# Two-layer transformer on one core: layer 1's weighted expert rows turned by DMA transposes of 16-bit halves instead of TensorE, with small moves of stores and copies between queues and steps

## The chip, the cores and the metric

The kernel runs on one core of one Trainium2 chip. The metric is the device time of one execution in microseconds, given as the median of several runs. One program holds both layers; nothing runs on the host.

## The reference

The input is x of shape (4, 512, 512): four sequences (b) of 512 rows, 2048 rows in all. Each of two layers computes a plain layernorm and adds two branches to x: attention and a mixture of experts, both fed by the normed rows.

```python
xn = layernorm(x)
x = x + L0_attn(xn) + L0_ffn(xn)
xn = layernorm(x)
x = x + L1_attn(xn) + L1_ffn(xn)
```

Layer 0's attention has 16 heads of 128. For each it makes queries and local keys (each normed and rotated), local values, a window of 128 keys and the block before it, and a sparse branch: every four rows are compressed to one entry, and each query takes the best 8 of the 128 compressed entries. Layer 0's experts: top 2 of 8, each a 512 x 512 product, weighted sum. Layer 1's attention is a plain softmax over 512 keys with 16 heads of 32. Layer 1's experts, which the main part of the change touches, end in a projection:

```python
h = einsum('td,edf->etf', xf, expert_w) + expert_b     # 8 experts, top 2 used
combined = sum of silu(h) of the two chosen experts, weighted by the softmax of their scores
out = combined @ proj_w + proj_b
y = x + out
return norm_w * y / sqrt(mean(y * y) + eps)            # x here is the normed xn
```

## The kernel before

All values are f32. The 2048 rows are 16 tiles n of 128 rows (NT = 16); 512 columns are four chunks of 128 (KC = 4). Each engine runs a fixed order of instructions. The order is found when the kernel is built, by a scheduler; instructions given to `keep_in_program_order` stay in the order in which the program issues them, the others may be moved. Transfers are issued from three engines' orders (SP, ACT, POOL); a transfer whose input is not ready holds everything behind it in that order. Tiles come from pools with a number of buffers each (`bufs`), and a new tile waits until the old one's users are done.

**Layer 0** runs in 32 steps of a pair of heads g and a sequence b. A step projects queries, keys and values (`p`, L734, through sums `u` on DVE), norms them (`squares`, L601 to L616), turns them for the products (trq L758, trk L772, trc L931 on TensorE, or stores of 16-bit halves `halves_q`, `halves_c` (L692), `halvesd_q`, `halvesd_c` (L698) and DMA transposes), then makes scores (L845, L856), contexts (L906 to L911, scaled by ACT at L922) and output products (L939, L970). Other work is hung into the steps by place: a list of pairs (step, place within it) and function, with places 0, 1, 2, 3, 3.5 and 4 in a step. Among it:

- Steps 2 to 4, preparation for layer 0's experts: `load_whole` loads a tile of normed rows (`xw`), `part_halves` copies it on ACT so that the low and the high 16-bit halves lie apart (`xh`, L1087), `store_parts` writes that to DRAM. [...]
- Steps 5 to 23, the experts: gathers of rows by POOL (L489, L524), stores (`xrd_r<-xr_r`, L529) and DMA transposes (`xT_r<-xrd_r`, L534), products `hp_r` (L552).
- Each step copies 16 KB of compressed entries (`cv0s`) at its head.
- Steps 29 to 31, `next_layer` for tiles 0 to 11: the rows of layer 1's layernorm (`xn`, L247) are stored (`xnd`, L250), POOL adds a bias to the residual `acc` (L1149), and `acc` is stored to DRAM (`accd`, L1150). Tiles 12 to 15 follow at the start of layer 1.

**Layer 1** runs in 64 slots (a row tile g and a quarter kc of the heads). A slot makes scores (L1522), exponentials on ACT (L1524), the product with the values (L1536), and part of the queries for a later tile (L1482, L1498). The experts lie over slots 9 to 47. From slot 48 on comes the mixing of tile n, one stage a slot, at slots s - 1 to s + 3 with s = 48 + 13 n // 16, so that tiles 0 and 1, 5 and 6, 10 and 11 share a slot:

- `fetch_mix`: POOL gathers the two experts' rows of each token, `g0` and `g1` (L569).
- `mix`: DVE weights and adds them (L1638, L1639) into `g0`.
- `turn_mix`: a load of the normed rows `xa` (L1645), four TensorE transposes `trc` (L1648), a load of the residual (`bring`, L1590), and an ACT copy into `combT` with a factor 0.5 (L1652).
- `project_mix`: four products `po` (L1660) of `combT` with the projection, DVE adds `xa` (L1661), ACT squares (L1664), POOL makes the root (L1665, L1666).
- `finish_mix`: DVE scales (L1671) and adds to the residual (L1594); SP stores to `out` (L1597), or to `accd` (L1599) where attention's part is still to come.

Of the kernel before, what the change touches and what calls it, by code (L numbers as in the profile page):

```python
# [12 lines left out]
F32 = mybir.dt.float32  # L13
# [37 lines left out]
def two_layers(ctx: ExitStack, tc: tile.TileContext, a: dict, out: bass.AP, large: bass.AP):  # L51
# [37 lines left out]
    def load_block(g, nm):  # L89


        w = wpool.tile([P, KC, 3 * D], F32, tag=nm, name=f"{nm}_{g}", bufs=1 if nm == "wA" else 2)
        for f in range(2):
            nc.sync.dma_start(out=w[:, ts(f, 2), :],
                              in_=a[nm][g, ts(f, 2 * P), :].rearrange("(k p) c -> p k c", p=P))
        return w
# [124 lines left out]
        tc.keep_in_program_order(V.memset(turned, 1.0))  # L221
        V.tensor_scalar(turned[R:P, :], wcol[R:P, 0:1], wcol[R:P, 1:2], D * math.sqrt(D), ALU.mult, ALU.mult)

    def layernorm(n, pool, bank, scaled=False, bufs=None):

        pin = tc.keep_in_program_order if n < TC else (lambda x: x)
        st = small.tile([P, 6], F32, tag="st", name=f"st_{n}")
        made_ = V.bn_stats(st, acc[:, n, :])  # L230
        if n < 2 * TC:
            tc.keep_in_program_order(made_)
        mv = small.tile([P, 2], F32, tag="mv", name=f"mv_{n}")
        V.bn_aggr(mv, st)
        V.tensor_scalar(mv[:, 1:2], mv[:, 1:2], 1e-5, None, ALU.add)
        G.tensor_tensor(mv[:, 1:2], mv[:, 1:2], nhalf[:, 0:1], ALU.pow)
        if scaled:
            G.tensor_scalar(mv[:, 0:1], mv[:, 0:1], mv[:, 1:2], -1.0, ALU.mult, ALU.mult)
        made = {}

        def rows():
            tag = "ctx" if n in (2, 3) else "xn"
            xn = made["xn"] = (wk0 if n in (2, 3) else pool).tile([P, HID], F32, tag=tag, name=f"xn_{n}", bufs=bufs)
            if scaled:
                pin(A.activation(xn, acc[:, n, :], AF.Identity, scale=mv[:, 1:2], bias=mv[:, 0:1]))
            else:
                made_ = V.tensor_scalar(xn, acc[:, n, :], mv[:, 0:1], mv[:, 1:2], ALU.subtract, ALU.mult)  # L247
                if n < TC or n + 1 == NT:
                    tc.keep_in_program_order(made_)
            (nc.scalar if TC <= n < 2 * TC else nc.sync).dma_start(out=xnd[ts(n, P), :], in_=xn)  # L250

        def turn():
            xn, tr = made["xn"], bank("tr", f"trx_{n}")
            for k in range(KC):
                made_ = pin(PE.transpose(tr[:, ts(k, P)], xn[:, ts(k, P)], ident))
                if n == TC + 1:
                    tc.keep_in_program_order(made_)
            pin(A.copy(xnT[:, :, ts(n, P)], tr.rearrange("p (k t) -> p k t", k=KC)))
        return rows, turn


# [205 lines left out]
    class Experts:  # L467
# [95 lines left out]
        def gather(self, n):  # L563

            rs = []
            for k in range(2):
                x = self.pool.tile([P, HID], F32, tag=f"row{k}", name=f"row{k}_{self.r.name}_{n}",
                                   bufs=(4, 3)[k] if self.silu else None)
                G.indirect_dma_start(out=x, out_offset=None, in_=self.yd,  # L569
                                     in_offset=at_rows(self.r.slot[:, k, n : n + 1]))  # L570
                rs.append(x)
            return rs
# [17 lines left out]
    for t_ in cv0s:  # L590
        G.memset(t_, 0.0)
        G.memset(t_[96:P, D : D + 1], 2.0)

    def squares(x, heads, pool, name, extra=1.0, use="k"):

# [482 lines left out]
    whole = {}  # L1078

    def load_whole(n):  # L1080
        x = whole[n] = rout["halves"].tile([P, HID], F32, tag="xw", name=f"xw_{n}", bufs=4)
        nc.sync.dma_start(out=x, in_=xnd[ts(n, P), :])

    def part_halves(n):
        x = whole[n]
        xh = whole[n] = rout["halves"].tile([P, 2, HID], U16, tag="xh", name=f"xh_{n}", bufs=4)
        A.copy(xh, x.bitcast(U16).rearrange("p (d h) -> p h d", h=2))  # L1087

    def store_parts(n):
        tc.keep_in_program_order(nc.sync.dma_start(out=xhd[ts(n, P)], in_=whole.pop(n)))  # L1090
# [29 lines left out]
    for b, place in enumerate(((3, 4), (4, 0), (4, 1), (4, 2), (4, 3))):  # L1120
        if b:
            jobs0.append((place, lambda b=b: rout["r"].list(b - 1)))
        if b < B:
            jobs0.append((place, lambda b=b: rout["r"].mark(b)))
    there = [(2, 4)] + [(3, h) for h in (0, 1, 2, 3, 3.5, 4)] + [(4, h) for h in (0, 1, 2)]
    for n in range(NT):
        k = n // 2
        for d, f in enumerate((load_whole, part_halves, store_parts)):
            jobs0.append((there[k + d], lambda n=n, f=f: f(n)))
    jobs0.append(((4, 3), begin_experts))  # L1130
    jobs0.append(((4, 3.5), lambda: rout["ex"].store_halves(0)))
    jobs0.append(((4, 3.5), lambda: rout["ex"].fetch_halves(1)))
# [8 lines left out]
            jobs0.append((at[2 * i + 1], lambda i=i: rout["ex"].fetch(i + 1)))  # L1141
        jobs0.append((at[2 * i + 1], lambda i=i: rout["ex"].store_halves(i + 2)))
    def next_layer(n, pool, bank):
        make_rows, turn_ = layernorm(n, pool, bank, bufs=2 if bank is psum else TC)

        def rows():
            make_rows()

            G.tensor_tensor(acc[:, n, :], acc[:, n, :], rout["wo_b"], ALU.add)  # L1149
            nc.sync.dma_start(out=accd[ts(n, P), :], in_=acc[:, n, :])  # L1150
        return rows, turn_

    v = {}
# [132 lines left out]
    for i, (g, b) in enumerate(steps):  # L1286
# [6 lines left out]
        turn_last = turn_keys  # L1293
        now = qkT
        cT = qp.tile([P, HG, S], F32, tag="cT", name=f"cT_{g}_{b}", bufs=1)
        nc.sync.dma_start(out=cv0s[i % 2][96:P, 0:D], in_=cv[0:32, b, 0:D])
        em0, lT0 = scores(i, 0, now, (lambda: (turn_last(1), next(comp[0]))) if i == 0 else None)
        if i:
            turn_last(1)
        if more:  # L1300
            load_sums(i + 1)
            qkT, sums_x, first, second, third, fourth, fifth, turn_queries, turn_keys, _ = project(i + 1)
            first()
            sums_x()
            if b == 2 and g + 1 in groups:
                groups[g + 1][0][0] = load_block(g + 1, "wA")
        run0((i, 0))
        em1, lT1 = scores(i, 1, now)
        if i == 0:
# [313 lines left out]
    def begin_mixing():  # L1623
        scratch.close()
        rout["mix"] = scratch.enter_context(tc.tile_pool(reuse_waits="tile", name="mix", bufs=2, side="right"))
        rout["ex1"].pool = rout["mix"]
        load_square(rout["mix"], "pw")
        for nm in ("pb", "nw1"):
            rows[nm] = load(rout["mix"], nm, [P, HID], a[nm].partition_broadcast(P))

    def fetch_mix(n):

# [2 lines left out]
    def mix(n):  # L1635

        g0, g1 = held[n]
        tc.keep_in_program_order(V.tensor_scalar(g0, g0, r1.gate[:, 0, n : n + 1], None, ALU.mult))  # L1638
        V.scalar_tensor_tensor(g0, g1, r1.gate[:, 1, n : n + 1], g0, ALU.mult, ALU.add)  # L1639
        held[n] = g0  # L1640

    def turn_mix(n):
        g0 = held[n]
        x = rout["mix"].tile([P, HID], F32, tag="xr", name=f"xa_{n}", bufs=4)
        nc.sync.dma_start(out=x, in_=xnd[ts(n, P), :])  # L1645
        tr = bank1("mm", f"trc_{n}")
        for f in range(KC):
            PE.transpose(tr[:, ts(f, P)], g0[:, ts(f, P)], ident)  # L1648
        bring(n, 1)
        cT_ = rout["mix"].tile([P, KC, P], F32, tag="xT", name=f"combT_{n}", bufs=3)  # L1650

        A.activation(cT_, tr.rearrange("p (k t) -> p k t", k=KC), AF.Copy, scale=0.5)  # L1652
        held[n] = cT_, x

    def project_mix(n):
# [833 lines left out]
```

## Time and profile before

| | us |
|---|---|
| median of 3 runs | 1981.68 |
| lowest, highest | 1981.44, 1984.95 |
| profiled execution, its own time | 1975.01 |
| its span in the profile | 1973.2 |

In the profiled execution TensorE's clock was 0.999 of full speed. Busy times of the stages that the change touches, from the windows of the trace:

| stretch, us | what runs | PE busy | ACT busy | DMA share |
|---|---|---|---|---|
| 160 to 210 | preparation of halves | 48.90 of 50 | 35.02 | 0.60 |
| 1290 to 1340 | end of layer 0 | 44.95 of 50 | 23.35 | 0.40 |
| 1870 to 1890 | mixing | 20.00 of 20 | 7.54 | 0.51 |

How to read the profile: PE is TensorE's products, PEld its weight loads beside them, DVE, ACT and POOL the other engines, SP only issues transfers. A group's row gives line, engine, operation, result and operands, count, then the busy time (overlaps of the group counted once), mean duration of one in ns, and the idle time of the engine ahead of the group with what ended it. A row of a timeline gives start, length, engine, line, operation and count, and in brackets the idle time before it with its releaser; SPq and ACTq rows are transfers as their queue issues them. A row of transfer issues ends with the median time from issue to landing.

### The profile page before, as it was taken

What the parts mean: (1) busy time and instruction counts of PE and PEld (TensorE: products, weight loads), DVE (VectorE), ACT (ScalarE), POOL (GpSimd) and SP (SyncE); (2) the same over time, 40 slices, a digit from 0 to 9 for tenths busy, and PEclk for the clock granted to TensorE, in tenths of its full rate; (3) what the DMA queues carried; (4) which work ended last, traced back from release to release, by engine and by line L of the source; (5) the groups of instructions that cost most, each with busy time, mean ns of one, the idle gap of its engine ahead of it and who ended that gap; (6) DMA issues with size and microseconds to landing.
All of it is one profiled execution on the core that took longest, in us unless ns stands there. A gap on an engine that the chain in (4) does not pass through costs nothing.

```text
span 1973.2 us, 28229 instructions
## 1 busy us (share of the span) xinstructions
PE 1933.4 (98%) x9010; PEld 1206.8 (61%) x9010; DVE 1481.5 (75%) x3662; ACT 892.8 (45%) x2650; POOL 756.1 (38%) x827
## 2 busy tenths in 40 slices
PE   7999999999999999999999999999999999999998
PEld 4676667776677677766667776666434445445443
DVE  7778878786776777776668888888796655666886
ACT  5556654444444444444445455455233433333332
POOL 5423244443433333344332454455114432333551
PEclk9999999999999999999999999999999999999999
DMA  9214366654666575567663433333317775775541
GB/s 293 104 61 142 130 176 180 198 155 144 186 191 167 172 204 152 147 184 223 221 223 98 121 109 109 95 113 105 122 53 257 256 256 191 277 251 175 158 154 67
DMA packets 224589, 326.51 MB, mean 165 GB/s; under 512 B 110384, under 2 KB 144304, under 8 KB 212656
## 3 DMA queue, kind: packets, MB, share of 16 engines
q1 hardware_dynamic: 196208, 173.60, 30.3%
q0 software_dynamic: 27072, 148.91, 22.4%
q10 hardware_dynamic: 1152, 2.10, 0.3%
q8 instruction: 74, 1.21, 0.3%
q14 instruction: 83, 0.68, 0.1%
HBM read 230.44 MB, written 70.25 MB: 152 GB/s over the span
## 4 chain that ended last, share of the span: by engine, by line
PE 79%; DVE 10%; DMA 4%; ACT 3%; issue 2%; POOL 1%; SPq 0%; DVEq 0%; ACTq 0%; POOLq 0%
PE p L734 23%; PE hp_r L552 12%; PE op L939 4%; PE st L856 4%; PE st L1522 3%; PE po L1660 3%; PE cx L1536 3%; PE qp L1498 3%; PE sp L845 2%; PE ox L970 2%; PE o L1605 2%; DMA halvesd_q<-halves_q 2%; PE oz L970 1%; PE ca L908 1%; PE trk L772 1%
## 5 line engine op out<-in xcount | busy, mean ns | idle before, releaser
L552 PE MATMUL hp_r<-we_r,xT_r 128*128 128x512 f32 (+1 forms) x592 | 226.4, 596 | 1.2 <-DMA we_r<-in_Wh,wrow_r 0.8
L606 POOL TENSOR_TENSOR ss_q<-ss_q,nhalf 128x4 f32<-128x4 f32 x64 | 70.9, 1108 | 375.0 <-ACT ss_q L603 375.0
L864 POOL TENSOR_TENSOR lT<-lT,lmask 128x512 f32<-128x512 f32 (+1 forms) x128 | 150.7, 1191 | 102.9 <-ACT lT L860 101.8
L734 PE MATMUL p<-wT,x 128*128 128x384 f32 x512 | 176.6, 488 | 2.6 <-DVE u L800 1.5
L734 PE MATMUL p<-wB,x 128*128 128x384 f32 x512 | 176.9, 490 | 1.3 <-DVE u L814 1.0
L734 PE MATMUL p<-wA,xnT 128*128 128x384 f32 x512 | 173.6, 490 | 1.0 <-DVE u L782 1.0
L860 ACT ACTIVATE lT<-st,ss_k 128x256 f32<-128x256 f32 (+1 forms) x256 | 98.8, 441 | 158.6 <-PE st L856 155.4
L1524 ACT ACTIVATE pT<-st 128x1024 f32<-128x1024 f32 x128 | 123.4, 1016 | 59.6 <-PE st L1522 51.1
L552 PEld LDWEIGHTS hp_r<-we_r,xT_r 128*128 128x128 f32 (+1 forms) x592 | 83.6, 170 | 98.2 <-issue 92.8
L734 PEld LDWEIGHTS p<-wB,x 128*128 128x128 f32 x512 | 94.0, 191 | 64.7 <-issue 8.8
L734 PEld LDWEIGHTS p<-wT,x 128*128 128x128 f32 x512 | 93.4, 190 | 64.9 <-DVE s L880 4.8
L734 PEld LDWEIGHTS p<-wA,xnT 128*128 128x128 f32 x512 | 95.1, 192 | 60.8 <-DVE u L782 2.8
L601 ACT ACTIVATE sq_q<-qb 128x128 f32<-128x128 f32 x256 | 79.2, 310 | 96.4 <-DVE qb L788 53.0
L856 PE MATMUL st<-qkT 128*128 128x256 f32 (+1 forms) x512 | 114.6, 353 | 0.0
L569 POOL DMA_INDIRECT row_r<-yd,slot_r x64 | 72.5, 1133 | 74.5 <-DMA yd<-yr_r 21.8
L856 PEld LDWEIGHTS st<-qkT 128*128 128x128 f32 x512 | 92.2, 190 | 11.5 <-issue 1.8
L939 PE MATMUL op<-Wo,cT 128*128 128x512 f32 x208 | 92.8, 593 | 0.0
L752 ACT ACTIVATE qb<-qb,ss_q 128x128 f32<-128x128 f32 x256 | 81.8, 392 | 21.3 <-POOL ss_k L605 16.0
L606 POOL TENSOR_TENSOR ss_k<-ss_k,nhalf 128x2 f32<-128x2 f32 (+1 forms) x96 | 86.7, 903 | 8.0
L734 PE MATMUL p<-wT,xnT 128*128 128x384 f32 x256 | 88.2, 487 | 0.3 <-DVE wT L121 0.3
L489 POOL DMA_INDIRECT xr_r<-xnd,rows_r x36 | 40.5, 1125 | 120.6 <-PE trm_r L540 88.4
L922 ACT ACTIVATE ctx<-cb,sums 128x128 f32<-128x128 f32 x128 | 39.7, 360 | 101.0 <-DVE sums L918 93.6
(390 smaller groups left out, 4558.5 us busy)
## 6 DMA issues: line engine op xcount, KB each, us to landing
x<-xsd SPq DMA_DIRECT2D x112, 256.0 KB, 5.1
yd<-yr_r SPq DMA_DIRECT2D x72, 256.0 KB, 5.4
xrd_r<-xr_r SPq DMA_DIRECT2D x36, 256.0 KB, 2.3
halvesd_c<-halves_c SPq DMA_DIRECT2D x27, 256.0 KB, 3.5
halvesd_q<-halves_q SPq DMA_DIRECT2D x26, 256.0 KB, 2.9
wA<-in_wA SPq DMA_DIRECT2D x16, 384.0 KB, 3.8
wB<-in_wB SPq DMA_DIRECT2D x16, 384.0 KB, 6.8
xnd<-xn SPq DMA_DIRECT2D x24, 256.0 KB, 2.0
```

The costliest lines, as they stand in the source:

```text
L552: PE.matmul(hp[ts(h, m), :], lhsT=xT[:, k, ts(h, m)], rhs=w[:, ts(k, HID)], start=(k == 0), stop=(k == KC - 1))
L569: G.indirect_dma_start(out=x, out_offset=None, in_=self.yd, in_offset=at_rows(self.r.slot[:, k, n : n + 1]))
L601: pin(A.activation(sq, x[:, h, :], AF.Square, accum_out=ss[:, j : j + 1]))
L606: pin(G.tensor_tensor(ss, ss, nhalf[:, 0:n], ALU.pow))
L734: fixed(PE.matmul(p, lhsT=x[:, k, ts(c, P)], rhs=w[:, k, :], start=(k == 0), stop=(k == 1)))
L752: A.activation(x[:, j, :], x[:, j, :], AF.Copy, scale=scale[:, n : n + 1])
L856: PE.matmul(st[:, ds((t % 2) * 256, n)], lhsT=qkT[:, HG + h, ts(t, P)], rhs=qkT[:, h, ds(t * P, n)], start=True, stop=True)
L860: A.activation(lT[:, ds(half * 512 + c * 256, n)], st[:, ds(c * 256, n)], AF.Exp, scale=norm_k[(i, h)][2 * half + c])
L864: G.tensor_tensor(dst, dst, lmask.rearrange("p a w j -> p (a w j)")[:, 0:n], ALU.mult)
L939: PE.matmul(op, lhsT=cT[:, h, ts(t, P)], rhs=wo[:, h, :], start=(h == 0), stop=(h == HG - 1))
L970: PE.matmul(p[:, ts(c, 256)], lhsT=left[:, ts(c, P)], rhs=right, start=new and c == 0, stop=True, skip_group_check=True)
L1524: A.activation(pt[:, ts(pair, 2), :], st, AF.Exp, scale=SCALE1)
```

## The change

1. The weighted rows of layer 1's experts are no longer turned by TensorE. `mix` copies `g0` on ACT into the buffer of `g1` with its 16-bit halves apart, and stores that to DRAM (`mhd`, two buffers) from SP. `turn_mix` issues a DMA transpose from there into `combT`. The factor 0.5 is put on the gates once. The second operation of the mix is kept in program order, and the numbers of buffers of the two gathered rows are swapped from 4 and 3 to 3 and 4.
2. The small copies of entries (`cv0s`) are issued a step ahead from step 5 on.
3. In `next_layer` for tiles 0 to 11 the stores of `xnd` and `accd` are issued from ScalarE's queue instead of SP's (for `xnd`, tiles 4 to 7 were there already).
4. The preparation of halves for layer 0's experts gets other places: tiles 0 to 5 in steps 1 and 2, in a pool of their own with two buffers, the rest from step 2 to step 4. The ACT copies are kept in program order.

```diff
@@ -221,7 +221,7 @@
         tc.keep_in_program_order(V.memset(turned, 1.0))
         V.tensor_scalar(turned[R:P, :], wcol[R:P, 0:1], wcol[R:P, 1:2], D * math.sqrt(D), ALU.mult, ALU.mult)
 
-    def layernorm(n, pool, bank, scaled=False, bufs=None):
+    def layernorm(n, pool, bank, scaled=False, bufs=None, on_scalar=False):
 
 
 
@@ -247,7 +247,7 @@
                 made_ = V.tensor_scalar(xn, acc[:, n, :], mv[:, 0:1], mv[:, 1:2], ALU.subtract, ALU.mult)
                 if n < TC or n + 1 == NT:
                     tc.keep_in_program_order(made_)
-            (nc.scalar if TC <= n < 2 * TC else nc.sync).dma_start(out=xnd[ts(n, P), :], in_=xn)
+            (nc.scalar if TC <= n < 2 * TC or on_scalar else nc.sync).dma_start(out=xnd[ts(n, P), :], in_=xn)
 
         def turn():
             xn, tr = made["xn"], bank("tr", f"trx_{n}")
@@ -565,7 +565,7 @@
             rs = []
             for k in range(2):
                 x = self.pool.tile([P, HID], F32, tag=f"row{k}", name=f"row{k}_{self.r.name}_{n}",
-                                   bufs=(4, 3)[k] if self.silu else None)
+                                   bufs=(3, 4)[k] if self.silu else None)
                 G.indirect_dma_start(out=x, out_offset=None, in_=self.yd,
                                      in_offset=at_rows(self.r.slot[:, k, n : n + 1]))
                 rs.append(x)
@@ -590,6 +590,9 @@
     for t_ in cv0s:
         G.memset(t_, 0.0)
         G.memset(t_[96:P, D : D + 1], 2.0)
+
+    def load_first_entries(i):
+        nc.sync.dma_start(out=cv0s[i % 2][96:P, 0:D], in_=cv[0:32, steps[i][1], 0:D])
 
     def squares(x, heads, pool, name, extra=1.0, use="k"):
 
@@ -1078,13 +1081,13 @@
     whole = {}
 
     def load_whole(n):
-        x = whole[n] = rout["halves"].tile([P, HID], F32, tag="xw", name=f"xw_{n}", bufs=4)
+        x = whole[n] = (rout["halves"] if n >= 6 else sp0).tile([P, HID], F32, tag="xw", name=f"xw_{n}", bufs=4 if n >= 6 else 2)
         nc.sync.dma_start(out=x, in_=xnd[ts(n, P), :])
 
     def part_halves(n):
         x = whole[n]
-        xh = whole[n] = rout["halves"].tile([P, 2, HID], U16, tag="xh", name=f"xh_{n}", bufs=4)
-        A.copy(xh, x.bitcast(U16).rearrange("p (d h) -> p h d", h=2))
+        xh = whole[n] = (rout["halves"] if n >= 6 else sp0).tile([P, 2, HID], U16, tag="xh", name=f"xh_{n}", bufs=4 if n >= 6 else 2)
+        tc.keep_in_program_order(A.copy(xh, x.bitcast(U16).rearrange("p (d h) -> p h d", h=2)))
 
     def store_parts(n):
         tc.keep_in_program_order(nc.sync.dma_start(out=xhd[ts(n, P)], in_=whole.pop(n)))
@@ -1122,11 +1125,11 @@
             jobs0.append((place, lambda b=b: rout["r"].list(b - 1)))
         if b < B:
             jobs0.append((place, lambda b=b: rout["r"].mark(b)))
-    there = [(2, 4)] + [(3, h) for h in (0, 1, 2, 3, 3.5, 4)] + [(4, h) for h in (0, 1, 2)]
+    there = [((1, 4), (2, 0), (2, 1)), ((2, 0), (2, 1), (2, 2)), ((2, 1), (2, 2), (2, 3)), ((2, 4), (3, 0), (3, 1)),
+             ((3, 0), (3, 1), (3, 2)), ((3, 1), (3, 2), (3, 3)), ((3, 4), (4, 0), (4, 1)), ((4, 0), (4, 1), (4, 2))]
     for n in range(NT):
-        k = n // 2
-        for d, f in enumerate((load_whole, part_halves, store_parts)):
-            jobs0.append((there[k + d], lambda n=n, f=f: f(n)))
+        for place, f in zip(there[n // 2], (load_whole, part_halves, store_parts)):
+            jobs0.append((place, lambda n=n, f=f: f(n)))
     jobs0.append(((4, 3), begin_experts))
     jobs0.append(((4, 3.5), lambda: rout["ex"].store_halves(0)))
     jobs0.append(((4, 3.5), lambda: rout["ex"].fetch_halves(1)))
@@ -1141,13 +1144,13 @@
             jobs0.append((at[2 * i + 1], lambda i=i: rout["ex"].fetch(i + 1)))
         jobs0.append((at[2 * i + 1], lambda i=i: rout["ex"].store_halves(i + 2)))
     def next_layer(n, pool, bank):
-        make_rows, turn_ = layernorm(n, pool, bank, bufs=2 if bank is psum else TC)
+        make_rows, turn_ = layernorm(n, pool, bank, bufs=2 if bank is psum else TC, on_scalar=bank is psum)
 
         def rows():
             make_rows()
 
             G.tensor_tensor(acc[:, n, :], acc[:, n, :], rout["wo_b"], ALU.add)
-            nc.sync.dma_start(out=accd[ts(n, P), :], in_=acc[:, n, :])
+            (nc.scalar if bank is psum else nc.sync).dma_start(out=accd[ts(n, P), :], in_=acc[:, n, :])
         return rows, turn_
 
     v = {}
@@ -1293,7 +1296,8 @@
         turn_last = turn_keys
         now = qkT
         cT = qp.tile([P, HG, S], F32, tag="cT", name=f"cT_{g}_{b}", bufs=1)
-        nc.sync.dma_start(out=cv0s[i % 2][96:P, 0:D], in_=cv[0:32, b, 0:D])
+        if i < 5:
+            load_first_entries(i)
         em0, lT0 = scores(i, 0, now, (lambda: (turn_last(1), next(comp[0]))) if i == 0 else None)
         if i:
             turn_last(1)
@@ -1304,6 +1308,8 @@
             sums_x()
             if b == 2 and g + 1 in groups:
                 groups[g + 1][0][0] = load_block(g + 1, "wA")
+            if i >= 4:
+                load_first_entries(i + 1)
         run0((i, 0))
         em1, lT1 = scores(i, 1, now)
         if i == 0:
@@ -1627,6 +1633,7 @@
         load_square(rout["mix"], "pw")
         for nm in ("pb", "nw1"):
             rows[nm] = load(rout["mix"], nm, [P, HID], a[nm].partition_broadcast(P))
+        tc.keep_in_program_order(V.tensor_scalar(r1.gate, r1.gate, 0.5, None, ALU.mult))
 
     def fetch_mix(n):
 
@@ -1636,20 +1643,18 @@
 
         g0, g1 = held[n]
         tc.keep_in_program_order(V.tensor_scalar(g0, g0, r1.gate[:, 0, n : n + 1], None, ALU.mult))
-        V.scalar_tensor_tensor(g0, g1, r1.gate[:, 1, n : n + 1], g0, ALU.mult, ALU.add)
-        held[n] = g0
+        tc.keep_in_program_order(V.scalar_tensor_tensor(g0, g1, r1.gate[:, 1, n : n + 1], g0, ALU.mult, ALU.add))
+        h = g1.bitcast(U16).rearrange("p (h d) -> p h d", h=2)
+        tc.keep_in_program_order(A.copy(h, g0.bitcast(U16).rearrange("p (d h) -> p h d", h=2)))
+        held[n] = dram.tile([P, 2, HID], U16, tag="mhd", name=f"mhd_{n}", bufs=2)
+        tc.keep_in_program_order(nc.sync.dma_start(out=held[n], in_=h))
 
     def turn_mix(n):
-        g0 = held[n]
+        cT_ = rout["mix"].tile([P, KC, P], F32, tag="xT", name=f"combT_{n}", bufs=3)
+        tc.keep_in_program_order(nc.sync.dma_start_transpose(out=cT_.bitcast(U16), in_=held[n].rearrange("p h d -> (p h) d")))
         x = rout["mix"].tile([P, HID], F32, tag="xr", name=f"xa_{n}", bufs=4)
         nc.sync.dma_start(out=x, in_=xnd[ts(n, P), :])
-        tr = bank1("mm", f"trc_{n}")
-        for f in range(KC):
-            PE.transpose(tr[:, ts(f, P)], g0[:, ts(f, P)], ident)
         bring(n, 1)
-        cT_ = rout["mix"].tile([P, KC, P], F32, tag="xT", name=f"combT_{n}", bufs=3)
-
-        A.activation(cT_, tr.rearrange("p (k t) -> p k t", k=KC), AF.Copy, scale=0.5)
         held[n] = cT_, x
 
     def project_mix(n):
```

## The prediction

> **What bounds the kernel now.** I read the profile page first (engine shares and slices), then the waits, then the windows and the timelines of the four stretches that the edits touch: about 160 to 260 us (preparation of halves), 1290 to 1390 us (border of the layers), and 1815 to 1948 us (mixing).
>
> ```profile
> span 1973.2 us, 28229 instructions
> ...
> PE 1933.4 (98%) x9010; PEld 1206.8 (61%) x9010; DVE 1481.5 (75%) x3662; ACT 892.8 (45%) x2650; POOL 756.1 (38%) x827
> ...
> PE   7999999999999999999999999999999999999998
> ...
> PEclk9999999999999999999999999999999999999999
> ```
>
> TensorE (PE) has work in 98% of the span at full clock. Only 1973.2 - 1933.4 = 39.8 us are left without it, of which about 15 lie in the first slices and 7 in the last. So an edit can gain in two ways only: PE instructions fall out of a stretch where PE is full, or one of the few PE stalls closes. The chain of waits says the same (PE 79% of the span, the first layer's projection and experts ahead). Losses have no such limit: any operand that comes late becomes time. The windows show where PE is full:
>
> ```profile
> 160.00:210.00 50.00, 48.90 (x242) 33.50 (x241) 41.00 (x146) 35.02 (x100) 12.24 (x16) 1.00 0.60 186
> 210.00:260.00 50.00, 47.27 (x234) 32.00 (x235) 46.23 (x146) 26.90 (x95) 16.14 (x19) 0.97 0.31 102
> ...
> 1290.00:1340.00 50.00, 44.95 (x221) 31.07 (x220) 42.63 (x116) 23.35 (x77) 28.28 (x30) 1.00 0.40 122
> 1340.00:1390.00 50.00, 48.77 (x242) 31.33 (x241) 39.43 (x119) 23.46 (x72) 21.71 (x24) 1.00 0.47 143
> ...
> 1890.00:1910.00 20.00, 20.00 (x90) 9.50 (x89) 17.48 (x25) 7.17 (x13) 14.03 (x13) 1.00 0.62 200
> ```
>
> The second number is the length, then busy time of PE, weight loads, DVE, ACT, POOL; then clock and DMA share. PE lacks 3.8 us in the early stretch, 6.3 us at the border, nothing in mixing.
>
> **Part 1, the turn of the weighted rows.** Removed from PE are 64 transposes:
>
> ```profile
> L1648 PE MATMUL trc<-ident,row_r 128*128 128x128 f32 x64 | 9.3, 273 | 0.2 <-DVE qk L1511 0.2
> ```
>
> Their records overlap, so 64 x 273 ns would be too much. In the timeline a group of four starts at 1844.28 and the next line follows at 1844.81: 0.53 us. Ten single tiles at 0.53, two double ones at 0.96 and the first pair at 1.43 (with its 0.24 of idle) make 8.65 us. PE is full there, so all of it comes off if nothing else is late.
>
> What takes their place: per tile one ACT copy of 128x1024 16-bit words (1.05 us by the halves_q row, for the 0.59 us combT copy removed), one store of 256 KB, one DMA transpose. ACT gains 16 x 0.45 = 7 us at under 50% load and has idle of 5 to 6.5 us in each slot, so its load costs nothing; its copy now stands between the two exponentials of a slot and waits for DVE's mix, but the attend product uses the previous slot's exponentials, so some 8 us cover it. Cost appears where a product po (L1660) waits for combT. The nearest rows for the transfers are
>
> ```profile
> x<-xsd SPq DMA_DIRECT2D x112, 256.0 KB, 5.1
> ...
> xrd_r<-xr_r SPq DMA_DIRECT2D x36, 256.0 KB, 2.3
> ...
> xnd<-xn SPq DMA_DIRECT2D x24, 256.0 KB, 2.0
> ```
>
> and for the transposes of the same shape
>
> ```profile
> xT_r<-xrd_r SPq DMA_TRANSPOSE x36, 4.9
> ```
>
> of which single ones landed 3.2 us after issue where nothing else ran, 9.4 at worst. From mix to combT this is 1.05 + 2.0 + 3.2 = 6.3 us at least, 8.3 at the median of the transpose, with 0.3 for each issue. Between the end of the mix on DVE and po there are 12 to 13.5 us for single tiles in before, but 6.9 (n=0), 10.6 (n=5), 10.3 (n=10), 8.4, 6.8, 7.4 (n=13 to 15). The chain alone would mostly fit.
>
> It does not run alone: it is in SP's queue, and in the compiled order of the changed kernel most transposes of tile n stand behind the store of the finished tile n-2 (n-3 in places), which holds SP until DVE has finished that tile.
>
> ```profile
> 1853.88 0.34 SPq L1597 DMA_DIRECT2D out<-acc  x1
> ...
> 1863.49 0.34 SPq L1597 DMA_DIRECT2D out<-acc  x1
> ...
> 1902.23 0.34 SPq L1597 DMA_DIRECT2D out<-acc  x1
> ```
>
> From that issue to the start of po I count, in before: n=3 5.9, n=4 6.1, n=5 3.0 (1863.49 to 1866.48), n=7 8.0, n=8 5.1, n=9 7.1, n=10 3.0 (1902.23 to 1905.22), n=12 8.0, n=13 1.5 us (behind the accd stores of tiles 10 and 11, 1922.83 to 1924.36). Where a group of four or eight transposes lay between, 0.5 or 1.0 goes off. Needed are 0.4 of issue plus the landing L. With L = 3.2: n=5 and n=10 are 1.6 late each, n=13 2.1, n=0 0.8, n=14 0.4: 6.5 us. With L = 4.9: 3.3, 3.3, 3.8, 2.5 (n=0), 0.7 (n=8), about 1.5 (n=14, 15): 15 us. The DMA share in these places is 0.4 to 0.7, so I take the middle, 11 us. The second tile of a pair comes 1.4 us behind the first and po of the first takes that long: hidden. Net of part 1: 11 - 8.65 = +2.4 us (from -8.65, if DVE runs ahead and nothing is late, to +6.4).
>
> [...]
>
> The scaling of the gates (DVE, 128x32, once) is about 0.1 us on an engine that isn't the bound. Buffers of the gathered rows are swapped between g0 and g1; the one lent to the halves is held until the store has landed, some 4 us more than before, under a gather issued a slot ahead.
>
> **Part 2, small copies a step ahead.** In SP's compiled order they stand in the same place for steps 6 on as before; the only shift is that a DMA transpose of the experts' rows stands one load earlier. Zero, within 0.5 either way.
>
> **Part 3, stores of layer 1's rows by ScalarE's queue.** 8 xnd and 12 accd stores leave SP. What SP held up:
>
> ```profile
> 1290.01 1.05 ACT L692 COPY halves_q<-qb 128x1024 uint16<-128x1024 uint16 x1
> ...
> 1294.24 0.32 SPq L250 DMA_DIRECT2D xnd<-xn  x1
> 1296.58 0.32 SPq L1150 DMA_DIRECT2D accd<-acc  x1
> 1296.94 0.43 SPq L698 DMA_DIRECT2D halvesd_q<-halves_q  x1
> ...
> 1305.27 0.63 PE L255 MATMUL trx<-ident,xn 128*128 128x128 f32 x4 [3.55 <-DVE xn L247]
> ```
>
> halves_q is ready at 1291.06 and its store goes at 1296.94, behind accd, which waits for POOL (L1149). halves_c on ACT waits for that landing (1300.47, idle 2.58), ACT's squares come late, then DVE's qb and xn, and PE stands 3.55 us. The same happens once more at 1334.8 to 1337.5, after which PE stands 1.49 and 0.98 us. If the queue is free, up to 6.0 us close. Against that, ACT issues 20 stores more (about 0.33 us each in its queue, 6.6 us over 100 us) and each accd store holds ACT until POOL is done, e.g. from 1294.6 to 1296.6, with the context's scaling (1296.35 to 1297.4) queued behind it. Estimate -3 us; bounds -6 and +2. [...]
>
> **Part 4, halves of the first layer's rows.** The first six of 16 loads, copies and stores move from the 174 to 220 us bunch to steps 1 and 2. In before ACT is crowded by 1.05 us copies, and PE stands for it:
>
> ```profile
> 211.95 0.33 PE L931 MATMUL trc<-ident,ctx 128*128 128x128 f32 x1 [2.38 <-DVE ctx L924]
> ...
> 214.49 0.90 PE L772 MATMUL trk<-ident,qb 128*128 128x128 f32 x3 [0.58 <-ACT qkT L759]
> ```
>
> At most 3 to 3.8 us close; the copies are now pinned in ACT's order and may wait for their own load (1.0 us in all before), with PE's operands behind them. -1.5, bounds -3 and +2.
>
> **Sum:** +2.4 - 3 - 1.5 = -2.1, so 1975.0 becomes 1972.9 for the profiled execution (span plus 1.8 outside it). That execution lies 6.7 us under the median of the runs; I carry the difference over: 1981.7 - 2.1 = 1979.6. What a measurement of this kernel can tell from no change is about 0.2%, 4 us: this case is mostly "same".
>
> **Rivals.**
> A, the transfers are hidden. If L is 3.2 and DVE finishes tiles earlier relative to PE once it has slack (it is 70 to 88% busy there), 2 to 4 us of stalls remain: -5.5, with -3.5 at the border and -1.5 early: about -10, 1971.5. For it: DMA is not full, PE alone is. Against: SP's order fixes the transposes behind the stores, whatever DMA can do.
> C, slower: SP's queue becomes the pace of mixing. Beyond L = 5.5, tiles 3, 4 and 8 are late too, and each us of L costs 6 to 8 us; at L = 6 that is about 22 us of stalls, net +13 for part 1, +9 in all: 1990. It decides from L of about 4.9, where stalls of 15 us outweigh the 8.65 + 4.5 gained. Against: the median row was taken where transposes queue in groups. For: gathers, loads and stores share these us (DMA share up to 0.74). An ACT that waits for POOL at the border (+2 instead of -3) puts the middle case on this side as well.
> D, the change does not do what it says: part 2 does not in the compiled order (above); the others do.
>
> **Numbers.** Middle case 0.38 (its own range 1975 to 1985; 0.09 of it faster by over 0.2%, 0.26 same, 0.03 slower), A 0.31, C 0.31. Faster by over 0.2% 0.40, within 0.26, slower 0.34. The range takes in A down to 1968 and C up to 1991.
>
> **What would show it.** Right: no trc L1648; PE waits "po <- DMA combT" near tiles 5, 10, 13 of 1 to 4 us each, about 11 in all; SP's transposes issued just behind out stores; the 3.55 us stall at 1305 gone and halvesd_q issued at once; accd stores as ACT waits for POOL. A is right if po waits under 4 us in sum; C if over 15. Wrong altogether: new stalls of DVE or ACT between 160 and 260 us, a lower clock, or gathers late for their buffers.

## The result: 0.6% slower, and the profile after

| | us |
|---|---|
| median before, 5 runs | 1981.44 |
| median of the changed kernel, 5 runs | 1994.39 |
| ratio, with 95% interval | 1.0063 (1.0045 to 1.0082) |
| profiled execution of the changed kernel | 1992.94, its span 1991.1 |

The changed kernel is slower by 12.5 us (0.0063 x 1981). The page of the changed kernel, in the lines that answer to those shown of before:

```profile
span 1991.1 us, 28178 instructions
...
PE 1937.1 (97%) x8946; PEld 1201.8 (60%) x8946; DVE 1478.9 (74%) x3663; ACT 899.3 (45%) x2650; POOL 748.5 (38%) x827
...
PEclk9999999999999999999999999999999999999999
```

64 instructions left TensorE, and its busy time rose from 1933.4 to 1937.1 us. That is the first odd thing: the same products took longer. The slices of the clock row hide it (9 is 0.9 or more). The windows show it (length, then busy times of PE, PEld, DVE, ACT, POOL, then clock, DMA share, GB/s):

```profile
160.00:210.00 50.00, 49.74 (x247) 34.74 (x246) 43.69 (x159) 33.20 (x107) 14.40 (x18) 1.00 0.47 151
210.00:260.00 50.00, 49.23 (x242) 32.07 (x241) 46.01 (x141) 25.93 (x86) 15.43 (x17) 1.00 0.38 132
1290.00:1340.00 50.00, 45.17 (x200) 29.54 (x199) 41.99 (x113) 23.17 (x78) 25.32 (x27) 0.97 0.39 119
...
1830.00:1835.00 5.00, 3.30 (x4) 1.51 (x5) 3.62 (x4) 1.21 (x2) 1.89 (x1) 0.56 1.02 177
1835.00:1840.00 5.00, 5.00 (x10) 2.15 (x9) 1.66 (x3) 0.72 (x2) 1.07 (x2) 0.75 0.55 139
1875.00:1880.00 5.00, 4.47 (x7) 2.04 (x8) 3.31 (x4) 0.10 (x1) 1.73 (x2) 0.66 1.01 282
...
1920.00:1925.00 5.00, 5.00 (x10) 2.22 (x9) 2.45 (x4) 0.00 (x0) 1.25 (x1) 0.72 1.06 332
```

PE is now fuller between 160 and 260 us (98.97 of 100, before 96.17), about as before at the border, and in mixing it has lost work and, at three places, clock. The waits of PE in mixing, and the products that end the three longest:

```profile
PE po L1665 <- DMA combT<-mhd: 12.1, 4, 5.0
...
PE po L1665 <- ACT pT L1530: 5.5, 1, 5.5
```

```profile
1831.70 9.96 PE L1665 MATMUL po<-pw,combT 128*128 128x512 f32 x16 [5.55 <-ACT pT L1530]
...
1875.53 8.53 PE L1665 MATMUL po<-pw,combT 128*128 128x512 f32 x16 [3.91 <-DMA combT<-mhd]
...
1919.03 8.97 PE L1665 MATMUL po<-pw,combT 128*128 128x512 f32 x16 [5.00 <-DMA combT<-mhd]
```

These are tiles 0, 5 and 10, each the first of a pair. In before, the products of a pair took 7.13 us and had no such wait, here those of tiles 0 and 1:

```profile
1827.74 7.13 PE L1660 MATMUL po<-pw,combT 128*128 128x512 f32 x16
```

Tiles 13 and 14 of the changed kernel wait 2.52 and 0.71 us more. Setting the same TensorE instructions of the two traces side by side shows where the time went (changed minus before, in us after the start):

| up to | changed kernel behind before by |
|---|---|
| 150 us | +1.1 |
| 250 us | -3.6 |
| 500 us | -6.35 |
| 940 us | -6.4 |
| 1000 us | -2.8 (two clock dips, after waits that before has too, without a dip) |
| 1290 us | -2.9 |
| 1375 us | +0.1 (1.7 of it a dip to 0.66 from 1300 to 1305 us) |
| 1820 us | -0.3 |
| end | +17.6 |

So mixing alone costs 18 us. One thing about the trace of before has to be kept in mind: its clock was 0.999, with one short stretch of half clock (3.41 us). Of the 99 later runs of the same kernel one had that clock; the others had 0.991 to 0.998, and their times go with it, from 1972.4 us at 0.999 over 1980.4 (median) at 0.995 to 1986.6 at 0.991.

### The profile page after: what moved, and what is told of

Same layout as the page of the kernel before. It is cut to its first block, busy times and chain, and to the rows that moved or that the text cites. A ratio compares the mean times of both kernels' runs of the same rounds, so it can differ in the third digit from the quotient of the medians.

```text
span 1991.1 us, 28178 instructions
## 1 busy us (share of the span) xinstructions
PE 1937.1 (97%) x8946; PEld 1201.8 (60%) x8946; DVE 1478.9 (74%) x3663; ACT 899.3 (45%) x2650; POOL 748.5 (38%) x827
## 5 line engine op out<-in xcount | busy, mean ns | idle before, releaser
L859 PEld LDWEIGHTS st<-qkT 128*128 128x128 f32 x512 | 92.1, 190 | 12.5 <-issue 1.3
L755 ACT ACTIVATE qb<-qb,ss_q 128x128 f32<-128x128 f32 x256 | 81.8, 392 | 24.2 <-POOL ss_k L608 17.6
L608 POOL TENSOR_SCALAR ss_k<-ss_k 128x2 f32<-128x2 f32 (+1 forms) x96 | 34.1, 356 | 140.0 <-ACT sq_k L604 133.9
```

The lines of the kernel that those rows point to most:

```text
L755: A.activation(x[:, j, :], x[:, j, :], AF.Copy, scale=scale[:, n : n + 1])
L859: PE.matmul(st[:, ds((t % 2) * 256, n)], lhsT=qkT[:, HG + h, ts(t, P)], rhs=qkT[:, h, ds(t * P, n)], start=True, stop=True)
```

## Experiments

Medians and ratios, each against runs of the kernel before on the same chip:

| kernel | us | before, us | ratio (95% interval) |
|---|---|---|---|
| no_turn | 1975.75 | 1983.43 | 0.9965 (0.9952 to 0.9978) |
| turn_only | 1999.67 | 1983.43 | 1.0088 (1.0063 to 1.0113) |
| early_only | 1975.23 | 1983.43 | 0.9967 (0.9955 to 0.9980) |
| stores_only | 1983.86 | 1983.43 | 1.0002 (0.9990 to 1.0014) |
| ahead | 1981.20 | 1978.19 | 1.0017 (1.0002 to 1.0033) |
| early0 | 1974.94 | 1978.19 | 0.9978 (0.9962 to 0.9994) |
| hybrid | 1978.27 | 1978.19 | 1.0008 (0.9994 to 1.0022) |
| fill | 2000.08 | 1978.19 | 1.0115 (1.0093 to 1.0137) |
| no_gather | 1972.80 | 1978.82 | 0.9965 (0.9948 to 0.9981) |
| fill2 | 1989.77 | 1978.82 | 1.0048 (1.0028 to 1.0067) |
| singles | 1971.47 | 1978.82 | 0.9964 (0.9949 to 0.9980) |
| best | 1970.40 | 1979.57 | 0.9952 (0.9937 to 0.9968) |

### Which part costs what

no_turn is the changed kernel with part 1 undone; turn_only, early_only and stores_only put one part alone into the kernel before. The edits are those of the diff above: for no_turn

```diff
-        tc.keep_in_program_order(nc.sync.dma_start_transpose(out=cT_.bitcast(U16), in_=held[n].rearrange("p h d -> (p h) d")))
+        for f in range(KC):
+            PE.transpose(tr[:, ts(f, P)], g0[:, ts(f, P)], ident)
...
+        A.activation(cT_, tr.rearrange("p (k t) -> p k t", k=KC), AF.Copy, scale=0.5)
```

> The changed kernel with only the turn of layer 1's weighted rows given back to TensorE (64 transposes, 16 ACT copies); the other three parts stay. In the two traces the mixing stage alone moved from 0.3 us ahead of the kernel before to 17.6 us behind it. Theory (the loss is all in the mixing stage): about 18 us come back, so 1976 to 1978 us, 3 to 6 us under the kernel before; no PE wait on combT, TensorE full from 1815 to 1948 us. Rival (the loss is from the other parts or from the clock at large): stays above 1985 us.

> The kernel before with only the turn of the weighted rows by transfers. Theory: slower by about 18 us (1998 to 2001 us), with PE waits of some 17 us on combT at tiles 0, 5, 10, 13 and clock dips behind them, the same places as in the whole change. Rival (the parts act on each other, e.g. the earlier halves shift the transfers): slower by under 10 us.

> The kernel before with only the earlier places of the halves for layer 0's experts (and their copies in order). Theory: faster by 4 to 7 us (about 1975 to 1977 us), the stall of 2.38 us before trc at 212 us and the clock dip behind it gone. Rival (the 7.5 us gained before 470 us came from the small copies a step ahead or from chance): within 2 us of the kernel before.

> The kernel before with only the 20 stores at the border of the layers issued from ScalarE's queue. By the two traces: the stall before trx shrinks from 3.55 to about 2.2 us, but new stalls (about 1.7 before a projection at 1324 us, 0.7 before scores) come; net 0 to 3 us slower. Rival (the prediction's term): 3 us faster, the border's stalls closed.

Measured against before: part 1 +17.5 us, part 4 -6.5 us, part 3 +0.4 us (zero within its interval). The product of the three ratios is 1.0057, the whole change 1.0063: the parts add up. Part 2 was not tried alone; no_turn (parts 2, 3 and 4) leaves it about -1 us, uncertain by some 4. In the trace of turn_only TensorE waits at the same tiles (5.17, 4.23, 6.26, 2.41 and 0.97 us at 0, 5, 10, 13 and 14), and no_turn has none of these waits. So the losses are all in part 1.

Part 4 gave four times its estimate. The windows of before and of early_only at the old stall:

```profile
210.00:215.00 5.00, 2.27 (x14) 1.71 (x15) 4.37 (x26) 5.00 (x15) 1.85 (x3) 0.94 0.46 161
215.00:220.00 5.00, 5.00 (x16) 3.31 (x15) 4.62 (x15) 2.06 (x5) 0.00 (x0) 0.72 0.35 102
```

```profile
210.00:260.00 50.00, 49.23 (x243) 32.13 (x242) 46.18 (x145) 26.46 (x88) 15.43 (x17) 1.00 0.38 131
```

In before, PE waits 2.38 and 0.58 us there, 0.58 more at 271 us, and runs at 0.94 and 0.72 of its clock right behind: 5 x 0.06 + 5 x 0.28 = 1.7 us. All of it is gone in early_only: 5.2 us together, of the 6.5 measured.

Part 3 moved waits and did not remove them. In stores_only, SP's row of the queue first, then ACT's:

```profile
1297.01 0.39 SPq L698 DMA_DIRECT2D halvesd_q<-halves_q  x1
```

```profile
1302.52 0.33 ACTq L1150 DMA_DIRECT2D accd<-acc  x1
1302.94 0.63 ACT L922 ACTIVATE ctx<-cb,sums 128x128 f32<-128x128 f32 x2 [2.90 <-PE p L734]
```

halvesd_q goes at once, as hoped (ready at 1295.94 + 1.04). But now ACT stands at accd until POOL is done, with ctx behind it. Of the 2.90 us only the last 0.8 are accd's, since ctx's own operand (`sums`, on DVE) is done at 1302.18. At 1328.52 accd holds ACT again: lT (L860) starts 2.52 us behind the first of its scores (L856), 1.07 in before. The stall before trx shrinks only from 3.55 to 2.23 us, and a new one of 1.70 opens:

```profile
1309.87 0.92 PE L255 MATMUL trx<-ident,xn 128*128 128x128 f32 x4 [2.23 <-DVE xn L247]
...
1334.36 1.56 PE L734 MATMUL p<-wA,xnT 128*128 128x384 f32 x4 [1.70 <-DVE u L782]
```

```profile
1330.63 3.21 DVE L879 TENSOR_TENSOR rep<-s,rep 128x320 f32<-128x320 f32 x1
```

DVE's u waited behind L879, which took 3.21 us; in before it took 0.48 to 1.03 at the border. In stores_only, POOL ran two mask operations (L864, 2.22 us from 1331.26) back to back in just that time, delayed together behind ACT's wait for accd. L879 was long beside such operations elsewhere too: of its 64 executions in the trace of before, the 20 with no TENSOR_TENSOR of POOL beside them took 0.49 us at most, and the longest, 3.12 us, had 2.28 us of them beside it. In the changed kernel, which has part 3 as well, the execution at 1321.85 us (there L882) took 3.20 us with 2.26 us of them beside it. By what they lengthen it was not tried apart. In sum TensorE waits 6.4 us between 1290 and 1400 us in before and 6.2 in stores_only.

### SP's order, and tile 0

ahead issues the transposes at the head of the slot, ahead of the out stores; early0 also mixes tiles 0 and 1 one slot earlier; hybrid leaves those two on TensorE.

```diff
-    def turn_mix(n):
+    def turn_first(n):
         cT_ = rout["mix"].tile([P, KC, P], F32, tag="xT", name=f"combT_{n}", bufs=3)
         tc.keep_in_program_order(nc.sync.dma_start_transpose(...))
+        held[n] = cT_
...
+    for n in range(NT):
+        jobs1.append((at[first + n * 13 // 16 + 1], lambda n=n: turn_first(n)))
```

> The changed kernel with the 16 DMA transposes issued at the head of their slot, ahead of the store of the finished tile (same buffers, same stage for all else). Theory (SP's order holds the transposes until DVE has finished the tile n-2; the transfer itself would be in time): the PE waits at tiles 5, 10, 13, 14, 12.1 us, shrink to under 3 us, with the clock dips behind 5 and 10 (3.3 us); tile 0, where nothing finished stands ahead, keeps its 5.5 us and its dip. So 12 to 15 us under the changed kernel, 3 to 6 us under the kernel before. Rival (the transfers are slow from traffic, whatever the order): the waits move or stay, less than 5 us gained on the changed kernel.

> As ahead, and the mix of tiles 0 and 1 with its copy, store and transpose one slot earlier. Theory (tile 0's wait is the bare length of the chain, made longer by four gathers in flight): its 5.5 us and the dip of about 3 us go too; all 8.65 us of removed transposes show: 11 to 15 us under the kernel before (about 1969 to 1972 where before is 1983). Rival: DVE or ACT wait for the gathers of tiles 0 and 1 a slot earlier, and the exponentials behind them: no better than ahead.

> As ahead, but tiles 0 and 1 turned by TensorE as before (8 transposes, 2 ACT copies). Theory: no wait at tile 0, and 7.4 us of transposes saved (14 tiles x 0.53): 10 to 14 us under the kernel before. If it lies by more than 3 us from the run with the earlier mix, one of the two opens a stall of its own. Rival (tile 2's transpose then waits in its place): within 3 us of ahead.

ahead gained 9 us on the changed kernel (1.0063 to 1.0017), less than the 12 to 15 expected, and its trace contradicts the theory:

```profile
1877.78 9.94 PE L1669 MATMUL po<-pw,combT 128*128 128x512 f32 x16 [4.54 <-DMA combT<-mhd]
```

Tile 5 still waits 4.54 us although its transpose goes 3.4 us behind the store of its halves, with no other store between. (Its profiled execution is 11 us above its median, so its waits are at the high end.) So SP's order is only a part. early0 closed tile 0's wait, but tile 5 still stands 3.94 us, and the run is 4 us under before (0.9978) instead of the 11 to 15 expected. hybrid missed its 10 to 14 us altogether: waits of 1.83, 1.77, 0.74 and 2.36 us are left at tiles 5, 10, 11 and 14. What is late was then read from early0: its transposes of tiles 5 and 6 go at 1856.84 and 1858.17, and POOL's queue issues

```profile
1855.38 1.03 POOL L569 DMA_INDIRECT row_r<-yd,slot_r  x1 [0.16 <-issue]
1856.71 0.96 POOL L569 DMA_INDIRECT row_r<-yd,slot_r  x1 [0.30 <-issue]
1857.98 0.96 POOL L569 DMA_INDIRECT row_r<-yd,slot_r  x1 [0.30 <-issue]
1859.24 1.49 POOL L569 DMA_INDIRECT row_r<-yd,slot_r  x1 [0.30 <-issue]
```

four gathers between 1855 and 1861 us. The last line of the view of combT in early0 (landing, us, shortest, median, longest) is

```profile
DMA to landing us min/median/max: 3.4/3.9/8.5
```

By the program, a gather of tile n's first row needs the buffer of tile n - 3, which the ACT copy of halves frees. The two copies of a pair free two buffers at once, and POOL's queue, held at the first, lets four gathers go, just as the pair's transposes are issued. The next run tries whether these gathers are the cause.

### Gathers left out

no_gather is ahead with POOL filling the buffers instead of gathering from tile 3 on, so the mixed rows are not the experts' results.

```diff
+                if self.silu and n >= 3:
+                    G.memset(x, 0.5)
+                else:
                     G.indirect_dma_start(out=x, out_offset=None, in_=self.yd,
```

> The kernel with the transposes at the head of their slot (ahead), with POOL's gathers of the experts' rows left out from tile 3 on (26 of 32; POOL fills the buffers with a constant instead, so the mixed rows are not the experts' results). Theory (the transposes of a pair land late because the ACT copies of the pair release four gathers at that moment, which share the DMA engines with them: 8.5 us for one of the pair, 3.3 us for single tiles): the PE waits at tiles 5 and 10 and at 13 (4.5, 2.2, 2.4 us in ahead) fall to under 1 us each, and the transposes of pairs land within 3.5 to 5 us. Tile 0 keeps most of its wait. Rival (two transposes of a pair slow each other, or SP holds them): the waits at 5 and 10 stay over 2 us.

```profile
PE po L1672 <- DMA combT<-mhd: 2.6, 1, 2.6
...
PE po L1672 <- issue: 1.2, 1, 1.2
```

```profile
DMA to landing us min/median/max: 3.2/3.4/4.1
```

Tiles 5, 6, 10 and 11 have no wait, and no landing in the trace takes more than 4.1 us (8.5 in early0, 7.6 in ahead). So it is the gathers that make them late, and not that a pair's two transposes are in flight together. By what they do it, by the load on the DMA engines or otherwise, was not tried apart. The stores of the halves land sooner as well (last number, median us), in early0 and in no_gather:

```profile
mhd<-row_r SPq DMA_DIRECT2D x16, 256.0 KB, 3.5
```

```profile
mhd<-row_r SPq DMA_DIRECT2D x16, 256.0 KB, 2.0
```

Tile 0's wait fell from 5.25 to 1.20 us as well, more than expected: the gathers ahead of it (of tiles 3 to 5) were its cause too, so the profile's "ACT pT" as its releaser is not what held it. Tile 14's 2.59 us stay: there the chain is simply short of time (the 2.4 us of ahead that the expectation puts at tile 13 are tile 14's). The ratio is 0.9965, 10 us under ahead's.

### The clock behind a wait

fill and fill2 put products that are not part of the computation right ahead of po of tiles 0, 5, 10 and 13, in the wait. In fill's trace a product is two records and takes 0.87 us (tile 0's 12 are 24 records, from 1825.65 to 1836.05 us), so fill had twice the length meant.

```diff
+        for k in range({0: 6, 5: 4, 10: 5, 13: 2}.get(n, 0)):
+            tc.keep_in_program_order(PE.matmul(op, lhsT=wa["pw"][:, 0, 0:P], rhs=wa["pw"][:, 1, :], start=True, stop=True))
```

> The changed kernel with TensorE kept at work in the four long waits: 12, 9, 10 and 5 products of 128x512 (0.43 us apart, results overwritten) stand right ahead of po of tiles 0, 5, 10 and 13, some 15.5 us of work that is not part of the computation. Theory (behind each long wait the clock is granted at half for some 3 us, which cost 2.9, 1.4 and 1.9 us here): the work falls into the waits, the clock stays full at these places, and the time falls by 4 to 6 us in spite of it. Rival (the clock falls from load or by chance, not from the wait): no change, or longer by what of the filler outlasts the waits.

> The filler of the earlier run at half its length: 6, 4, 5 and 2 products (each takes 0.87 us at full clock, in two passes), 14.8 us of work that is not part of the computation, in waits of 5.5, 3.9, 5.0 and 2.5 us of the changed kernel. Theory (half clock behind each long wait): no dip at these places, the products behind them at 7.0 us for a pair instead of 8.5 to 10, and 4 to 6 us under the changed kernel, so at a ratio to the kernel before of about 1.004 instead of 1.0063. Rival: the same 1.006 or above.

fill was 10 us slower than the changed kernel (1.0115), as its filler of 31 us outlasted the waits of 17 us; its time tells nothing for or against, but all three pairs' products ran in 7.03 us. fill2's windows at the same places:

```profile
1830.00:1835.00 5.00, 4.60 (x11) 1.82 (x10) 4.22 (x5) 0.53 (x1) 1.76 (x1) 1.00 1.00 216
1835.00:1840.00 5.00, 5.00 (x24) 1.61 (x22) 2.20 (x4) 1.49 (x5) 1.69 (x3) 1.00 0.50 108
1872.00:1877.00 5.00, 4.32 (x10) 2.01 (x11) 4.97 (x6) 0.00 (x0) 1.47 (x2) 1.00 1.02 281
1915.00:1920.00 5.00, 5.00 (x13) 2.27 (x13) 4.38 (x6) 0.36 (x1) 1.26 (x1) 1.00 1.14 316
```

No dip; pairs run in 7.13 us instead of 9.96, 8.53 and 8.97 (6 us). In the traces mixing costs 12.6 us instead of 18.0, with 14.8 us more work for TensorE. The ratio fell from 1.0063 to 1.0048, 3 us; the intervals overlap, so the runs' times alone would not settle it. The clock does, in every run and not in the profiled one alone: its mean over an execution is 0.989 to 0.993 in the five runs of the changed kernel, 0.995 to 0.997 in the six of fill and 0.994 to 1.000 in the nine of fill2. fill2's first wait also ends, 0.40 us behind the filler, on combT: tile 0 was waiting for the transfer.

```profile
1831.22 7.13 PE L1667 MATMUL po<-pw,combT 128*128 128x512 f32 x16 [0.40 <-DMA combT<-mhd]
```

Which waits were followed by half clock can be read from the traces of before and of the changed kernel. From 15 us on and without the last 10 us, before has one stretch of half clock, at 214.39 us, and the changed kernel has seven, at 24.98, 939.75, 987.54, 1301.56, 1830.63, 1875.00 and 1915.96 us. These seven begin on one grid of 3.41 us and last one or two of its windows; in the windows of 5 us of eleven other traces (all but best's), from 20 to 1950 us, each stretch comes to 3.41 or 6.83 us too. Whether half clock follows goes here with the idle time of TensorE within one window. First before, then the changed kernel, cut along its own grid at the stall ahead of trx:

```profile
1299.83:1303.25 3.42, 1.88 (x14) 1.27 (x12) 0.69 (x4) 2.66 (x10) 0.00 (x0) 1.00 0.64 198
1303.25:1306.66 3.41, 1.39 (x7) 1.07 (x8) 2.21 (x9) 2.69 (x11) 3.06 (x4) 1.00 0.64 171
1306.66:1310.07 3.41, 3.41 (x12) 2.04 (x11) 3.41 (x10) 1.36 (x5) 2.05 (x3) 1.00 0.72 170
```

```profile
1298.15:1301.56 3.41, 1.18 (x8) 0.60 (x7) 1.81 (x6) 2.63 (x13) 2.15 (x4) 1.00 0.74 178
1301.56:1304.97 3.41, 3.41 (x8) 1.89 (x7) 1.04 (x6) 2.37 (x7) 1.69 (x2) 0.50 0.70 213
1304.97:1308.38 3.41, 3.41 (x15) 2.16 (x15) 2.98 (x8) 0.00 (x0) 0.00 (x0) 1.00 0.28 77
```

The stall of before is longer, 3.55 us, but the grid splits it into 1.53 and 2.02 us of idle time, and the clock stays full. That of the changed kernel, 2.23 us, lies within one window, and half clock follows for the next. Over these two traces, of the windows at full clock all 5 with more than 2.03 us of idle time (2.05 to 3.41) were followed by half clock, none of the 1123 with less than 1.65, and 3 of the 7 between. In the changed kernel half clock went on for a second window where the first had 1.07 us of idle time (tile 0) and 3.07 (tile 10), not where it had 0.53 (tile 5) or none (the other four). These are counts of two executions; what sets the clock was not tried apart. Tile 0's windows, the first of them wholly in its wait:

```profile
1827.22:1830.63 3.41, 0.00 (x0) 0.00 (x0) 3.41 (x5) 2.30 (x3) 0.24 (x2) 1.00 1.14 157
1830.63:1834.04 3.41, 2.34 (x3) 1.18 (x4) 2.99 (x3) 0.58 (x1) 1.81 (x1) 0.50 1.03 131
1834.04:1837.46 3.42, 3.42 (x5) 1.35 (x4) 0.00 (x0) 0.00 (x0) 0.81 (x1) 0.50 0.48 177
1837.46:1840.87 3.41, 3.41 (x9) 1.52 (x8) 1.89 (x3) 0.72 (x2) 0.89 (x3) 1.00 0.62 141
```

### A version from the findings

singles turns nine tiles by transfers: 0 and 1, mixed a slot earlier, and of the later ones those that share no slot. The two later pairs and the last three tiles stay on TensorE. best is the same without parts 2 and 3.

```diff
+    by_pe = (5, 6, 10, 11, 13, 14, 15)
...
+        if n in by_pe:
+            tr = bank1("mm", f"trc_{n}")
+            for f in range(KC):
+                PE.transpose(tr[:, ts(f, P)], cT_[:, ts(f, P)], ident)
```

> A version built from the findings: earlier halves kept; tiles 0 and 1 mixed a slot early; transposes at the head of the slot for tiles 0 to 4, 7, 8, 9 and 12; TensorE turns the tiles of the later pairs and the last three (5, 6, 10, 11, 13, 14, 15). Theory: no PE wait on combT over 0.7 us, 9 x 0.53 = 4.8 us of TensorE saved on top of the 6.5 us of the earlier halves: ratio 0.993 to 0.995, better than all before it. Rival (the gathers collide with single tiles as well): not under 0.9965, what the halves alone gave.

> The kernel before with two things only: the earlier places of the halves for layer 0's experts, and the mixing of the singles version (tiles 0 to 4, 7, 8, 9, 12 turned by transfers ahead of their slot's other stores, tiles 0 and 1 mixed a slot early, the rest on TensorE). The border's stores stay with SP and the small copies where they were. Theory (the border's change is worth nothing): like singles, ratio 0.994 to 0.997. Rival (the new stalls of 1.7 and 0.7 us at the border cost more than the closed one gives): 1 to 2 us better than singles.

In mixing PE waits 0.9 us in singles; in best the view of waits has no line for TensorE there. singles came out at 0.9964, short of the 0.993 to 0.995 expected and not better than early_only; best at 0.9952, 9.5 us under before, the lowest ratio of all. The intervals of best, singles and early_only overlap, so what the nine transfers add to the earlier halves (3 to 4 us in the traces' mixing stages) is likely, not shown by the runs. The kernel before and the changed one are both slower than best.

## Why the prediction was wrong

The forecast was 1979.6 us, "same" or faster, and the range ended at 1991; 1994.4 came. The side and the sign of case C (slower, po waits over 15 us) came true, with a chance of 0.34 for slower. Its picture did not: tiles 3, 4 and 8, late in it, do not wait on combT.

- *PE is the bound, and losses have no limit.* Right.
- *"All of it comes off", 8.65 us.* A little too much. From a single tile to the next po gains 0.44 us on before (6.36 us behind at tile 2, 5.92 at tile 3; 10.01 at tile 7, 9.58 at tile 8), not 0.53: the next products had overlapped the last transpose. Over 16 tiles that is 7 us.
- *Landing L between 3.2 and 4.9, "I take the middle, 11 us".* This is the step that failed. The kind of wait was right, its size was not: 17.7 us. Tile 0 waits 5.55 us (0.8 to 2.5 in the prediction), tiles 5 and 10 wait 3.91 and 5.00 (1.6 to 3.3 each); tile 13, with 2.52, is as foreseen. From the issue of the transpose to po it takes 8.0 us at tile 0 and 4.4 and 5.3 at tiles 5 and 10, with gathers of later tiles in flight (at tile 5 that is still within the prediction's L, and the shorter lead, below, did the rest). Leaving these out closes the waits at 5 and 10 and leaves 1.2 us at tile 0 (no_gather, with the transposes ahead in SP's order). The prediction had a gather's buffers in view and set them to nothing: the one lent to the halves is held longer, "under a gather issued a slot ahead". The gathers were not ahead; they were waiting for buffers that the copies and stores of the halves free, and went with the transposes.
- *SP's order holds the transposes.* Right as a reading (tiles 5, 10, 13 were among the late ones), and the lead was even shorter than counted: at tiles 5 and 10 the store of the finished tile goes 0.9 and 0.7 us ahead of the moment when PE is free for po, where the prediction has 2.0 (3.0 less the eight transposes). Removing this order bought 9 us, but the pair kept its wait.
- *No term for the clock.* The prediction took full clock for given; a lower one stands only among its signs of being wrong altogether. Behind the three longest waits the same products took 6.1 us more (2.8, 1.4 and 1.8 over 7.13). With the waits, 23.8 us, less 7 us of removed transposes, makes 17 of the 18 us. The 6.7 us by which the profiled execution of before lies under the median, carried over as they were, are of the same kind: by the later runs a clock of 0.995 instead of 0.999 costs some 8 us.
- *Part 3, -3 us.* Zero (+0.4 us in stores_only). The bound of +2 was for a wait moved to ACT, and that happened: the wait in SP's order was real and went away, and ACT's came for it.
- *Part 4, -1.5 us with at most -3.8.* -6.5 us measured. Its stalls were seen, the 1.7 us of half clock behind one of them was not counted, though the window's 0.97 was among the lines shown.
- *Part 2, zero.* Not contradicted.
- *The turn by transfers.* It lost at the pairs that meet the gathers (5.55, 3.91 and 5.00 us of waits at tiles 0, 5 and 10). For the nine tiles that best turns by transfers TensorE has no wait.

Forecast (-2.1 us) and measured time (+12.5) lie 14.6 us apart: 6.7 of waits, 6.1 of clock, 1.7 of transposes and 3.4 of part 3, less 5.0 of part 4, make 12.9; the rest is within the interval of the ratio.

## What to carry to other kernels

When a stage moves from a full engine to transfers, list what the new instructions release, not only what they wait for: here the copies that free the gathers' buffers started four gathers just as a pair's transposes went, and the longest landing was 8.5 us (early0), and 4.1 without the gathers (no_gather). On a kernel bound by TensorE, price a wait of 2 us or more above its length, since half clock may follow it (here 1.4 to 2.8 us more). The wait of 3.55 us in before, split by the grid into 1.53 and 2.02, cost nothing more; how long a wait can be for that was not shown. Look at windows of 5 us, since a row of 40 slices hides it (0.56 in a window here, 9 in every slice), and at the clock of the profiled execution before carrying its time over to a median. A store moved to another engine's queue can take its wait along: here accd's held ACT, and lT came 2.52 us behind its scores instead of 1.07.

## What the runs showed of the hardware that was not expected

- Behind a wait TensorE ran at half clock for 3.41 or 6.83 us (0.56 and 0.75 in two windows of 5 us), at a cost of 1.4 to 2.8 us. The length of the wait alone did not tell whether it would: in before, the wait of 3.55 us at 1302 us is followed by full clock, and one of 2.38 at 210 us by 0.72; the changed kernel's waits of 2.05 and 2.15 us at 936 and 984 us were followed by 0.68 and 0.75, where before waited 1.77 and 2.17 at the same instructions at full clock. In these two traces it went with the idle time within one window of a grid of 3.41 us: half clock followed all five windows with 2.05 to 3.41 us of it, and neither of the two, with 1.53 and 2.02, that the wait of 3.55 us fell into.
- DMA transposes of 256 KB (an f32 tile, which the program hands over as 16-bit halves) landed in 3.2 to 4.1 us with the gathers from tile 3 on left out (no_gather), and in up to 7.6 (ahead) and 8.5 us (early0) with them.
- A DVE operation on two tensors (L879, 128x320) took 0.49 us at most with no TENSOR_TENSOR of POOL at the same time (20 executions in before), 3.12 us beside 2.28 us of them (before) and 3.20 beside 2.26 (the changed kernel).
